# A graph network's first layer in one pass over a symmetric adjacency, with its batch norms as affine maps

## The chip, the cores and the metric

The kernel runs on one core of a Trainium2 chip. The metric is the time on the device in microseconds (us), the median of several executions. The engines are named as in the profile: PE multiplies matrices (PEld is its loading of weights), DVE is the vector engine, ACT the scalar engine, POOL GpSimd, and SP the engine that issues most of the DMA transfers. Each engine works through its own instructions in a fixed order and waits on semaphores for the others.

## The reference, cut to what matters

There are B = 16 batches of N = 1024 nodes with D = 128 features. `adj` is a matrix of 0 and 1 for each batch; it is drawn at random, made symmetric, and has ones on its diagonal. Four layers follow each other; each ends in a residual and a layer norm over the features.

```python
# layer 0
w = masked_row_softmax(transpose(adj))       # equal shares over the neighbours
region = w @ x
region = batch_norm(region @ kernel_1 + bias_1)      # over batches and nodes, 256 features
people = transpose(w) @ region
people = batch_norm(people @ kernel_2 + bias_2)      # over batches and nodes, 128 features
x = layernorm(x + people)
# layer 1: h = x @ W + b_W;  e[i,j] = leaky_relu(s1[i] + s2[j] + b_a)
#          softmax over i of where(adj > 0, e), relu, residual, layer norm
# layers 2, 3: scores[i,j] = leaky_relu(sum_d h[i,d] a[d] h[j,d]) where adj == 1,
#              softmax over j, times h, residual, layer norm
```

Because the entries are 0 and 1, the softmax of layer 0 gives 1/degree at each neighbour. The batch norms need the mean and variance over all 16 batches before any batch can go on.

## The kernel before

`fast_path` computes all four layers; a flag `bad`, gathered from checks on the data (that adj holds 0 and 1 only, and that the sums of the softmaxes lie in bounds), starts `general_path` if one fails. The order of each engine's queue is fixed when the program is built: a scheduler walks through the operations in the order in which the Python code calls them, with the buffers and PSUM slots of the tile pools deciding what can stand early. In the names, C = 8 is the number of 128-row blocks of a batch, H = 2 and G = 2 are halves of 512 columns and groups of four blocks, and A = 129.

Layer 0 takes two sweeps over the batches. In the first, each batch loads x (L510), splits it into a high and a low half in the matmul's rounded type (L512 on ACT, L513 on DVE), loads eight rows of adj of 512 KB (SP) and casts them to a mask `m` (`cast_mask`: every third on ACT, L461, the others on DVE, L463). 64 matmuls (L523) with blocks of the mask as weights add up the neighbours of each node, the degree in one more column; L526 to L530 divide, L535 transposes, L536 copies into `hid`, which stays in SBUF for all batches, and L540 and L542 take the statistics of the first batch norm. `batch_norm_affine` turns them into a scale and a shift, which are folded into one matrix `k12` and one row `c12` (L544 to L565). In the second sweep each batch forms `hid` times `k12` (L574), adds and divides (L577, L579), splits again (L583, L584), loads eight rows of `adjt`, the transpose of adj laid out on the host, casts them to a mask, and sums with 32 matmuls of 512 columns (L593). `people` goes to DRAM, transposed, with a bias (L598, statistics L600, store L601 on ACT's queue). The second batch norm follows.

Layers 1 to 3 are in the class `Batch`. Even batches form one stream and odd ones another, three phases behind; the phases `first`, `first_sum`, `other`, `other_sum`, `other`, `other_sum` of the two streams are laced together by the position of each step in its phase. Buffers carry the stream's number, and most exist once per stream, `x0` among them. The phase `first` is the entry of layer 1:

- `load` (L676, L678): x0 and the batch's people, `pe`, from DRAM;
- `people_norm` (L681): the second batch norm as one ACT operation on the transposed people;
- `add_transposed` (L657, L658): eight transposes on PE into PSUM, two additions on DVE with x0 into `res`; `collect` (L637, L638) takes the moments of each of the eight blocks;
- `apply`: the layer norm. `rsqrt` has two operations on POOL (L443, L444), then L644 on DVE and eight ACT operations L648; `rows_of` transposes the result (L667, L669);
- `scores1` (L695, L696, L697), `values1` (L706, L708, L711) and eight steps `weights1`, each with a row of `adjt` from DRAM (L715), ACT's L717 and DVE's L721 and L723.

Beside it runs, in the other stream, an `other_sum` or `other` phase with its matmuls L758 or L748 and the exponentials L753.

## Time and profile before

| | |
|---|---|
| time, median of 3 (range) | 2398.34 us (2398.07 to 2401.47) |
| time of the profiled execution | 2401.34 us |
| its span | 2399.5 us |
| busy PE, DVE, ACT, POOL | 78%, 68%, 41%, 6% of the span |
| granted PE clock, mean | 0.891 |
| 0 to 270 us: PE, DVE, ACT busy; DMA share; GB/s | 228.05, 194.09, 109.45 us; 0.89; 305 |
| 270 to 480 us: the same | 172.06, 137.60, 70.15 us; 0.94; 339 |
| read from memory, written | 226.90 MB, 16.78 MB |

The page cuts the span into 40 equal slices of 60 us; a digit is the busy share in tenths. The slices of the DMA row separate layer 0 from the rest. A row of the timeline gives the start in us, the busy time, the engine and line, the operation with its output and inputs, the tile's shape, how many instructions the row holds, and in brackets how long the engine had been idle and what released it. PE's ends are modelled, so the duration of one matmul is best taken from the distance between neighbours in a row of many.

### The profile page before, as it was taken

How to read it: one execution, taken by the hardware profiler on the slowest of the kernel's cores; microseconds unless marked ns; L12 is line 12 of the kernel's file. 1: busy time of each engine (PE TensorE's matmuls, PEld its weight loads, DVE VectorE, ACT ScalarE, POOL GpSimd, SP SyncE). 2: the span in 40 equal slices, each digit the busy share in tenths (PEclk: the TensorE clock that was granted, in tenths of full speed). 3: DMA queues.
4: the chain of work that ended last, by engine and by line, in shares of the span. 5: the costliest groups of instructions: out<-in, count | busy, mean ns of one | idle time of the engine just before them, and what ended most of it. 6: DMA issues, size and time to landing. Idle time of an engine off the chain costs nothing.

```text
span 2399.5 us, 24698 instructions
## 1 busy us (share of the span) xinstructions
PE 1874.0 (78%) x8661; PEld 1255.8 (52%) x8661; DVE 1626.4 (68%) x3714; ACT 981.9 (41%) x1577; POOL 150.5 (6%) x220
## 2 busy tenths in 40 slices
PE   6999888647787877868696969696868787878786
PEld 5776765425363645454554545454545454645464
DVE  5777776546575858575857676676758585767664
ACT  3444333333444444444444344444434343535332
POOL 0000000000000000000101010100000000000000
PEclk9999999968888989898888989898989898889887
DMA  8999899931111212020203030303030202020100
GB/s 288 315 309 319 281 343 359 347 118 39 49 54 43 64 33 79 19 76 22 88 9 97 1 97 0 97 1 97 1 97 14 84 27 70 9 71 10 44 9 11
DMA packets 110951, 245.39 MB, mean 102 GB/s; under 512 B 7776, under 2 KB 57568, under 8 KB 110816
## 3 DMA queue, kind: packets, MB, share of 16 engines
q1 hardware_dynamic: 108512, 235.31, 29.2%
q10 hardware_dynamic: 2304, 8.39, 0.9%
q8 instruction: 71, 1.16, 0.2%
q14 instruction: 64, 0.52, 0.1%
HBM read 226.90 MB, written 16.78 MB: 102 GB/s over the span
## 4 chain that ended last, share of the span: by engine, by line
DVE 44%; PE 30%; ACT 9%; DMA 6%; issue 5%; POOL 4%; SPq 0%; ACTq 0%; POOLq 0%
PE pacc L737 10%; PE pbig L748 4%; DMA at<-in_adjt_dram 4%; DVE ln_st L637 4%; PE pz L523 4%; PE pacc L758 3%; DVE m L463 2%; PE pt L667 2%; PE pr L540 2%; PE pbig L695 1%; PE pacc L706 1%; POOL rs_t L443 1%; PE pz L593 1%; DVE rs L763 1%; DMA at<-in_adj_dram 1%
## 5 line engine op out<-in xcount | busy, mean ns | idle before, releaser
L523 PE MATMUL pz<-x,m 128*128 128x258 f32 x1024 | 163.1, 307 | 27.9 <-DVE reg L530 18.1
L463 DVE CAST m<-at 128x1024 fp32r<-128x1024 int32 x192 | 131.2, 684 | 73.4 <-DMA at<-in_adjt_dram 58.7
L523 PEld LDWEIGHTS pz<-x,m 128*128 128x128 f32 x1024 | 137.8, 199 | 52.3 <-DVE reg L530 26.2
L593 PE MATMUL pz<-m,x 128*128 128x512 f32 x512 | 144.9, 419 | 25.6 <-DVE m L463 15.7
L762 DVE TENSOR_SCALAR sums<-pacc 128x1 f32<-128x1 f32 x256 | 37.7, 147 | 150.5 <-PE pacc L758 149.2
L593 PEld LDWEIGHTS pz<-m,x 128*128 128x128 f32 x512 | 92.0, 194 | 66.0 <-DVE m L463 33.1
L461 ACT CAST m<-at 128x1024 fp32r<-128x1024 int32 x64 | 67.0, 1047 | 71.3 <-DMA at<-in_adjt_dram 69.0
L529 ACT ACTIVATE lo<-pz,rdeg 128x128 f32<-128x128 f32 x128 | 42.0, 366 | 106.6 <-DVE degs L526 74.6
L542 DVE BATCH_NORM_STATS2 stats<-pr 128x6 f32<-128x512 f32 x64 | 44.5, 696 | 30.7 <-PE pr L540 30.7
L540 PE MATMUL pr<-hid,k_sb 128*128 128x512 f32 x128 | 64.9, 618 | 0.3 <-ACT hid L536 0.3
L530 DVE SCALAR_TENSOR_TENSOR reg<-pz,rdeg,lo 128x128 f32<-128x128 f32 x128 | 40.5, 346 | 8.9 <-ACT lo L529 8.5
L598 ACT ACTIVATE reg<-pz,vec 128x512 f32<-128x512 f32 x32 | 20.2, 684 | 62.0 <-PE pz L593 62.0
L574 PE MATMUL pr<-k,hid 128*128 128x128 f32 x256 | 37.6, 290 | 7.6 <-DVE xf L577 7.6
L763 DVE RECIPROCAL rs<-sums 128x1 f32<-128x1 f32 x256 | 40.2, 159 | 4.7
L574 PEld LDWEIGHTS pr<-k,hid 128*128 128x128 f32 x256 | 35.7, 202 | 13.3 <-issue 7.0
L751 DVE TENSOR_TENSOR e__4340<-pbig,pen__4339 128x1024 f32<-128x1024 f32 x16 | 19.1, 1211 | 26.4 <-PE pbig L748 26.4
L737 PE MATMUL pacc<-e__4340,hn__4348 128*128 128x512 f32 x32 | 15.8, 655 | 21.4 <-DVE hn__4348 L730 21.4
L536 ACT COPY hid<-zt 128x512 f32<-128x512 f32 x32 | 18.7, 586 | 33.5 <-PE zt L535 33.5
L751 DVE TENSOR_TENSOR e__6601<-pbig,pen__6600 128x1024 f32<-128x1024 f32 x16 | 19.2, 1206 | 19.0 <-PE pbig L748 19.0
L751 DVE TENSOR_TENSOR e__5325<-pbig,pen__5324 128x1024 f32<-128x1024 f32 x16 | 19.2, 1205 | 18.9 <-PE pbig L748 18.9
L751 DVE TENSOR_TENSOR e__9153<-pbig,pen__9152 128x1024 f32<-128x1024 f32 x16 | 19.2, 1203 | 18.8 <-PE pbig L748 18.8
L751 DVE TENSOR_TENSOR e__10429<-pbig,pen__10428 128x1024 f32<-128x1024 f32 x16 | 19.2, 1203 | 18.7 <-PE pbig L748 18.7
(1313 smaller groups left out, 5057.2 us busy)
## 6 DMA issues: line engine op xcount, KB each, us to landing
at<-in_adj_dram SPq DMA_DIRECT2D x128, 512.0 KB, 5.8
at<-in_adjt_dram SPq DMA_DIRECT2D x128, 512.0 KB, 5.6
adjt<-in_adjt_dram SPq DMA_DIRECT2D x128, 512.0 KB, 3.6
xf<-in_x_dram SPq DMA_DIRECT2D x16, 512.0 KB, 7.6
people<-reg ACTq DMA_DIRECT2D x16, 512.0 KB, 6.0
x__4267<-in_x_dram SPq DMA_DIRECT2D x1, 512.0 KB, 4.5
x__4548<-in_x_dram SPq DMA_DIRECT2D x1, 512.0 KB, 6.8
pe__4269<-people SPq DMA_DIRECT2D x1, 512.0 KB, 3.3
```

Source lines behind the costliest of these rows:

```text
L461: nc.scalar.copy(dst, src)
L463: nc.vector.tensor_copy(dst, src)
L523: nc.tensor.matmul(pz[:, :2 * D + 2], m[:, i, j * P:(j + 1) * P], x2[:, i, :], start=(i == 0), stop=(i == C - 1))
L540: nc.tensor.matmul(pr, k1_sb[:, s * P:(s + 1) * P], hid[b][:, h * 512:(h + 1) * 512], start=True, stop=True)
L574: nc.tensor.matmul(pv[:, k * P:(k + 1) * P], hid[b][:, c * P:(c + 1) * P], k12, start=True, stop=True)
L593: nc.tensor.matmul(pp[h], v2[:, c, s, :], mt[:, c, h * 512:(h + 1) * 512], start=(c == 0 and s == 0), stop=(c == C - 1 and s == 1))
L637: nc.vector.bn_stats(st, self.res[:, c, :])
L737: nc.tensor.matmul(po, self.hn[:, c, :D], self.e[:, c, h * 512:(h + 1) * 512], start=(c == 0), stop=(c == C - 1))
L748: nc.tensor.matmul(ps[:, cols], self.xw[:, c * P:(c + 1) * P], self.xt[:, cols], start=True, stop=True)
L751: nc.vector.tensor_tensor(e, ps, self.pen[:, c, :], ALU.subtract)
L758: nc.tensor.matmul(po[:, :A], self.e[:, m, c * P:(c + 1) * P], self.xl[:, m, :], start=(m == 0), stop=(m == C - 1))
L763: nc.vector.reciprocal(rs, total)
```

## The change

Layer 0 becomes one pass over adj, in a class `Pass` with two phases per batch; the second phase of a batch is laced with the first of the next one by `in_turn`.

The first phase loads x and splits it as before, loads the eight rows of adj and casts each on ACT, where the same operation sums the row into `degs`. The mask is now what is streamed (32 matmuls of 512 columns, into two PSUM tiles `z`), so that the sums come out transposed. `compare` checks on the chip that adj is symmetric: 36 blocks per batch are transposed by a matmul with an identity, and DVE counts the elements in which they differ from the mirrored block (12 operations). A difference would make `bad` start the general path.

The second phase copies z to SBUF, transposes it back and divides by the degrees (`region`), multiplies the region by its own transpose into a running PSUM sum (`moment1`), divides once more and splits (`split`), and sums over the neighbours with 64 matmuls of 258 columns which use the same mask (`back`). The result `g` (129 columns: the 128 features and the sum of the weights) takes part in a second running sum (`moment2`) and goes to DRAM.

Since kernel_1, the batch norms and kernel_2 are affine maps, they are applied after the sums: when all batches are through, the covariance of the regions gives the first norm's scale and shift, the moments of g the second's, and all of it becomes a matrix `k12s`, a row `c12s` and a row `shift2s`. At the entry of layer 1 each batch loads g, POOL adds `shift2s` to x0, g is transposed (`people_rows`) and multiplied by `k12s`, and `add_people` adds the product and g's last column times `c12s` to x0. `people_norm` and the transposes of `pe` are gone.

```diff
-    people = dram.tile([B, P, N], F32, name="people")
+    people = dram.tile([B, P, C, A + 1], F32, name="people")
...
+    def affine(scale, shift, var, mean, gamma, beta):
...
+    with tc.tile_pool(name="z_load", bufs=4) as zl, tc.tile_pool(name="z_mask", bufs=3) as zm, \
+            tc.tile_pool(name="z_work", bufs=2) as zw, \
+            tc.tile_pool(name="z_sum", bufs=1, space=PSUM) as zs, \
+            tc.tile_pool(name="z_acc", bufs=2, space=PSUM) as za, \
+            tc.tile_pool(name="z_tr", bufs=2, space=PSUM) as zt, \
+            tc.tile_pool(name="z_gram", bufs=1, space=PSUM) as zg:
...
+            def add(self, i):
+                at = zl.tile([P, N], I32, name="at")
+                nc.sync.dma_start(at, adj[self.b, i * P:(i + 1) * P, :])
+                nc.scalar.activation(self.m[:, i, :], at, AF.Copy,
+                                     accum_out=degs[:, self.b, i:i + 1])
+                for s in range(2):
+                    for h in range(H):
+                        nc.tensor.matmul(self.z[h], self.x2[:, i, s, :],
+                                         self.m[:, i, h * 512:(h + 1) * 512],
+                                         start=(i == 0 and s == 0), stop=(i == C - 1 and s == 1))
+            def compare(self, j):
+                for k0 in range(0, j + 1, 4):
+                    n = min(4, j + 1 - k0)
+                    pt = zt.tile([P, 512], F32, name="zt")
+                    for k in range(n):
+                        nc.tensor.matmul(pt[:, k * P:(k + 1) * P],
+                                         self.m[:, k0 + k, j * P:(j + 1) * P], identr,
+                                         start=True, stop=True)
+                    junk = zw.tile([P, 512], BF16, name="junk")
+                    nc.vector.scalar_tensor_tensor(
+                        junk[:, :n * P], pt[:, :n * P], 1.0,
+                        self.m[:, j, k0 * P:(k0 + n) * P].bitcast(F32), ALU.mult, ALU.not_equal,
+                        accum_out=unlike[:, self.b, j, k0 // 4:k0 // 4 + 1])
+            def rows(self):
...
+                for h in range(H):
+                    nc.scalar.copy(self.zt[:, h * 512:(h + 1) * 512], self.z[h])
...
+            def region(self, g):
...
+            def moment1(self, c):
+                nc.tensor.matmul(moments1[:, :A + 1], self.reg[:, c, :D], self.reg[:, c, :],
+                                 start=(self.b == 0 and c == 0),
+                                 stop=(self.b == B - 1 and c == C - 1))
+            def split(self):
...
+            def back(self, c):
+                pz = za.tile([P, 512], F32, name="pz")
+                for j in range(C):
+                    nc.tensor.matmul(pz[:, :2 * A], self.m[:, j, c * P:(c + 1) * P],
+                                     self.v2[:, j].rearrange("p s a -> p (s a)"),
+                                     start=(j == 0), stop=(j == C - 1))
+                lo = zw.tile([P, A], F32, name="lo")
+                nc.scalar.copy(lo, pz[:, A:2 * A])
+                nc.vector.tensor_tensor(self.g[:, c, :A], pz[:, :A], lo, ALU.add)
...
+            def store(self):
+                nc.vector.bn_stats(wstats[:, self.b, :], self.g[:, :, D])
+                nc.scalar.dma_start(people[self.b], self.g)
...
+        last = []
+        for b in range(B + 1):
+            first, second = Pass(b).phases() if b < B else ([], [])
+            in_turn(last, first)
+            last = second
...
             def load(self):
                 self.x0 = self.tile(rows, [P, C, D], F32, "x0")
                 nc.sync.dma_start(self.x0, x[self.b].rearrange("(c p) d -> p c d", p=P))
-                self.pe = self.row("pe")
-                nc.sync.dma_start(self.pe, people[self.b])
-
-            def people_norm(self):
-                nc.scalar.activation(self.pe, self.pe, AF.Identity, bias=shift2, scale=scale2)
+                self.g = self.tile(rows, [P, C, A + 1], F32, "g")
+                nc.sync.dma_start(self.g, people[self.b])
+                nc.gpsimd.tensor_tensor(
+                    self.x0, self.x0, wide["shift2s"][:, None, :].to_broadcast([P, C, D]), ALU.add)
                 self.new_norm()
+                self.gt = self.row("xt")
+
+            def people_rows(self, g):
+                pt = ps_tr.tile([P, 512], F32, name="pt")
+                for k in range(4):
+                    nc.tensor.transpose(pt[:, k * P:(k + 1) * P], self.g[:, 4 * g + k, :D], ident)
+                nc.scalar.copy(self.gt[:, g * 512:(g + 1) * 512], pt)
+
+            def add_people(self, g):
+                pt = ps_tr.tile([P, 4, P], F32, name="pt")
+                for k in range(4):
+                    c = 4 * g + k
+                    nc.tensor.matmul(pt[:, k, :], self.gt[:, c * P:(c + 1) * P], wide["k12s"],
+                                     start=True, stop=True)
+                    nc.vector.scalar_tensor_tensor(self.x0[:, c, :], wide["c12s"],
+                                                   self.g[:, c, D:A], self.x0[:, c, :], ALU.mult,
+                                                   ALU.add)
+                nc.vector.tensor_add(self.res[:, 4 * g:4 * g + 4, :], pt,
+                                     self.x0[:, 4 * g:4 * g + 4, :])
+                for k in range(4):
+                    self.collect(4 * g + k)
```

In the changed file the new lines of layer 0 are L505 (cast with degrees), L509 (z), L519 and L523 (`compare`), L535 (copies of z), L543 and L545 (`region`), L550 and L577 (the two running sums), L557, L560 and L561 (`split`), L569, L573 and L574 (`back`), L582 and L583 (`store`), L632 to L732 (the affine maps). At the entry of layer 1 they are L800 and L802 (loads), L803 (POOL's add), L811 and L812 (`people_rows`), L818, L820 and L823 (`add_people`). Later lines only move: L443 and L444 keep their numbers, L648 becomes L772, L695 becomes L839, L706 L850, L708 L852, L753 L897, L758 L902.

## The prediction

> **What bounds the kernel now.** I read the page's slices first, then the table of stretches, then the timeline of one cycle of each stage, and last the DMA issues.
>
> ```profile
> span 2399.5 us, 24698 instructions
> PE   6999888647787877868696969696868787878786
> DVE  5777776546575858575857676676758585767664
> PEclk9999999968888989898888989898989898889887
> DMA  8999899931111212020203030303030202020100
> ```
>
> The DMA row splits the span: eight slices (480 us, layer 0) at eight or nine tenths, then almost none. The stretches say the same; the columns are the stretch, its length, busy time of PE, PEld, DVE, ACT and POOL, granted clock, DMA share and GB/s.
>
> ```profile
> 120.00:180.00 60.00, 54.46 (x316) 42.11 (x316) 45.33 (x141) 26.15 (x52) 0.45 (x4) 0.97 0.91 309
> 360.00:420.00 60.00, 48.77 (x218) 34.05 (x219) 38.86 (x58) 18.22 (x21) 0.00 (x0) 1.00 0.97 358
> 800.00:1000.00 200.00, 155.62 (x689) 99.76 (x688) 136.96 (x314) 84.13 (x135) 16.50 (x22) 0.89 0.18 58
> ```
>
> So layer 0 is paid twice for the adjacency at 91 to 97% of the DMA engines (about 30 us per batch, both sweeps), with PE close behind. Layers 1 to 3 have a free DMA, and PE 78% and DVE 68% busy: no engine is full, so hand-overs between in-order queues bound them. One of these hand-overs is what the change touches, at the entry of layer 1 of an even batch:
>
> ```profile
> 924.00 2.28 ACT L753 ACTIVATE e__5963<-e__5963,shift 128x1024 f32<-128x1024 f32 x2 [0.30 <-DVE e__5963 L752]
> 925.01 1.28 DVE L658 TENSOR_TENSOR res__6469<-pt,x__6462 128x512 f32<-128x512 f32 x2
> 926.32 0.38 SPq L676 DMA_DIRECT2D x__7738<-in_x_dram  x1
> 929.78 0.20 POOL L443 TENSOR_SCALAR rs_t<-ln_mv__6470 128x8 f32<-128x8 f32 x1 [2.40 <-DVE ln_mv__6470 L638]
> 930.06 1.64 POOL L444 TENSOR_TENSOR ln_rstd__6523<-rs_t,neg_half 128x8 f32<-128x8 f32 x1
> 932.07 3.19 ACT L648 ACTIVATE xl__6529<-res__6469,ln_off__6527,ln_rstd__6523 128x128 f32<-128x128 f32 x8 [1.57 <-DVE rs L763]
> 935.77 1.98 PE L695 MATMUL pbig<-xt__6555,wa_rep 128*128 128x512 f32 x4
> 938.46 1.79 DVE L708 TENSOR_TENSOR hn__6609<-pacc,bw_row 128x387 f32<-128x387 f32 x3 [3.08 <-PE pacc L706]
> ...
> 1052.68 3.78 PE L695 MATMUL pbig<-xt__7193,wa_rep 128*128 128x512 f32 x4
> ```
>
> The reader is to see a single chain: residual (L658, ends 926.29), moments, POOL's rsqrt (L443, L444), ACT's apply (L648), PE (L695), DVE (L708, after 3.08 us idle). DVE and PE have nothing else in front in their queues, so a late L443 moves everything. The last row is the same four matmuls at half the granted clock: 3.78 us against 1.98. And the load of the x of the batch after next in this stream goes out at 926.32, the moment L658 has freed the buffer (one x0 buffer per stream).
>
> **Part 1, the loop of layer 0.** Removed: 128 loads of 512 KB (67 MB; at 339 GB/s some 200 us of transfer), the second casts, L535, L540, L574. Added: symmetry test (36 matmuls, 12 DVE operations per batch) and gram matrices. DMA per batch falls to 8 rows, x and people: ten times 1.66 us (512 KB at 315 GB/s), about 16.6 us. PE per batch, from the spacing inside rows of one group:
>
> ```profile
> 137.20 2.19 PE L523 MATMUL pz<-x,m 128*128 128x258 f32 x16
> 299.89 2.84 PE L574 MATMUL pr<-k,hid 128*128 128x128 f32 x24
> 309.38 9.56 PE L593 MATMUL pz<-m,x 128*128 128x512 f32 x38
> ```
>
> 258 columns: .127; 512: .248; fp32 of 128 columns: two instructions of .112, .224. Not in the trace is an fp32r 128x128 matmul on its own; bounds .063 (.127 halved with the columns) and .224 (fp32); I take the transposes' .11 (L535). 32x.248 + 64x.127 + 36x.11 + 8x.11 + 16x.224 = 24.5 us (23.5 with median spacings). ACT: 8 casts with accumulated degrees, for which L717 (1024 columns, accumulated) issues every 1.13 us, beside plain casts of 1.05 and 1.33 with the read-out not overlapped; I take 1.14: 9.1, plus x and v casts 2.1, z copies 1.2, eight lo .37: 17 us. DVE 14.5. So PE's sum is the floor, not DMA's.
>
> But batch b+1's sums and batch b's second phase are laced in fixed queues, and I follow the hand-overs. In the built program's queues, after z is summed: z copies .59+.59 (L536's row) and the x cast 1.06 on ACT; on DVE the low half of x 1.23 stands ahead of the last comparison's .75, and region's second group needs the PSUM slot which that comparison holds; two regions .68+.68 (L577's row), a comparison .35, v 1.23, ACT's v copy 1.05, low half of v 1.22: 9.4, with some .5 of semaphores 9.9. Then PE: 64 back matmuls 8.13, 7 z matmuls 1.74, 9 comparison matmuls .99: with .28 of fill 11.1. Then ACT, whose last five casts stand behind the last lo: .37 + 5x1.14 + .33 (people's issue), the last with a row that is only asked for when the fourth buffer is free: 6.5 to 7.5 before the next z copy. Sum 27.5 us per batch; the bounds are the dense floor 23.5 and, with the comparisons at .224, the casts at 1.33 and .2 more per hand-over, 30.5.
>
> First z copy: first cast 9.9 us, then DMA and eight rows, 27.5. Then 15x27.5 = 412, 440. Tail: no next batch to lace (regions to v 7.6, back 8.1, lo and moment2 1.5, less 3): 454. The batch-norm chains behind the last gram matrix are some 45 dependent small operations, .16 to .56 each (DVE .16, POOL .56 by L444's one-column row, PE fp32 about .43) : 15 to 17.5; 471. Store and first loads of people lie beside these. L811 to L823 (eight transposes, two .59 copies, eight .224 matmuls, add): 6.5, so the first residual is done at about 478, against
>
> ```profile
> 488.31 0.69 DVE L658 TENSOR_TENSOR res__4272<-pt,x__4267 128x512 f32<-128x512 f32 x1 [8.82 <-PE pt L657]
> ```
>
> Gain 10 us; ends -61 (23.5 per batch) and +35 (30.5).
>
> **Part 2, the entry of layer 1.** Removed per batch: people_norm on ACT 1.24 and 8 transposes. Added: L811, two copies of .59, eight matmuls of .224, eight DVE operations L820 (nearest L530 .35, L557 .28; 2.4 us in all) and one POOL add over 128x1024 (L803). L820 I cost at nothing: DVE idles 1.89, 1.09 and 3.08 us in the stretch shown; were that cover gone, 16x2.4 = 38 us.
>
> L803 is the matter. The add for batch b+2 stands in POOL's queue ahead of batch b's own L443, for b = 1, 2, 4, 6, 8, 10, 12. It waits for the load of x, which waits for batch b's L823 to free the buffer. So L443 of b waits for: L823 (its copies stand before the two last exponentials, whose sum matmuls stand before L818: 926.28 + two copies 1.18 + four sums .71 + the last four L818 .9 + the add .66 + some .6 of semaphores = 930.3 instead of 926.29, +4.1); the load, 4.65 by this row
>
> ```profile
> x__7738<-in_x_dram SPq DMA_DIRECT2D x1, 512.0 KB, 4.7
> ```
>
> (bounds 3.9 and 5.3, the other x loads); the add. No row shows a POOL add of this size: lower bound L513 on DVE, 1.2; upper 3.3, twice the whole of L444, POOL's longest; I take 2.3, between, as POOL's small operations run .20 to 1.64 where DVE's run .16 to .17. Against the present 3.5 from L658's end to L443: 4.1 + 4.65 + 2.3 - 3.5 = 7.6. PE's idle grows by as much, so L695 and L706 behind it go at half clock, some 1.6 of the row above's 1.8; one sum group fewer on DVE behind it saves 1.1. Per batch 7.5 to 8, seven batches 52 to 57. The last even batch, 14, has no b+2: +3. Odd ones (7) put the copies and matmuls beside sums: .5 each, 3.5. Layers 1 to 3: +59.
>
> The Trainium skill's "GPSIMD Engine Reference", section 3.1, measures a two-input add of 2048 fp32 columns at 4497 ns on GpSimd against 2293 on VectorE; halved, an estimate of 2.25 us for L803, and it speaks against the placement. No run here shows it yet. "TensorE: Matmul & The Clock Gate", Part 1, has the half clock come after about 3.4 us of idle; by that rule the wait of L443 costs clock as well as time, and so might the 9.9 us of hand-overs in each cycle of layer 0.
>
> **Sum.** 59 - 10 = +49. The profiled execution took 2401.34 us (span 2399.5 and 1.8 around it), 3.0 above the median of 2398.34; so 2450 for its like, 2447 against the median. Own range 2425 to 2475.
>
> **Rivals.**
> Faster: layer 0 becomes dense on PE. If the laced matmuls fill the 9.9 us, the cycle is 23.5 and saves 60 more: 2387. It decides from a cycle of 24.2 us (27.5 - 49/15) down. For it: PE is 54.46 of 60 busy in sweep one today; against it: region needs z whole and PE may run only three rows ahead. Chance .17.
>
> PE drops to half clock in every cycle of layer 0: the wait before the back matmuls holds some 4 us of PE work in 9.9. Price, one slow stretch of 1.7 to 3.4, 2.5x15 = 38: 2485. Chance .15. Against: clock 0.97 today.
>
> The POOL wait is mostly hidden (x lands early, or other work is drawn forward): 3 instead of 7.6 per batch, 21+6.5-10: 2416. Chance .15. Against: queues are in order and DVE's gaps show nothing to draw.
>
> The symmetry test fails and the general path runs: its loads alone, four times 67 MB at 343 GB/s, are 780 us: over 3200. Chance .01; adj is made symmetric with ones on the diagonal.
>
> **Chances and range.** Forecast .52, rivals as given. Faster by over 0.2% (5 us, what a measurement of this kernel can tell from none) .17: the first rival; same .04, from edges of it and the third; slower .79. The range 2385 to 2495 takes in all but the farthest of the first two rivals and the last.
>
> **What would show it.** Layer 0: z copies 27.5 us apart, PE share there about 85%, DMA share near 0.55, first L823 near 478. Entry: L803 right ahead of L443 with its releaser the x load, L443 about 7 to 8 us later after L823 than L658 now, L839 at about 3.8 us. Wrong if z copies come every 24 us, if L443 does not wait for L803, or if L820 shows on the chain.

## The result and the profile after

The changed kernel takes 2461.73 us (median of 4, 2460.2 to 2463.38) against 2398.72 us of the kernel before on the same chip: a ratio of 1.0261, 95% interval 1.0243 to 1.0278. It is slower by 63 us; 2447 were forecast, within 2385 to 2495. The profiled execution took 2463.38 us, its span 2461.6.

The slices of the page, as before in 40 parts, now of 61.5 us:

```profile
span 2461.6 us, 26764 instructions
PE   7898999566968686868686868686868687878786
DVE  4545555456767676767576757675767575857674
PEclk9999999677989797979797979797979797989887
DMA  9656542122020202020202020202020202020100
```

The reader should see that the DMA row falls to 5 and 4 within layer 0, that PE stands at 9 there, and that layer 0 is hardly shorter. DVE's digits in layer 0 fall to 4 and 5, since the casts have gone to ACT.

Where the time went is read from the first residual of layer 1 (L658 before, L823 after), which divides the span. Rows of the timeline:

```profile
471.58 0.68 DVE L823 TENSOR_TENSOR res__4758<-pt,x__4753 128x512 f32<-128x512 f32 x1
```

It came at 488.31 before and comes at 471.58 now. Layer 0 and its affine maps thus give back 16.7 us; what follows takes 2461.6 - 471.6 = 1990.0 instead of 1911.2, which is 78.8 more. The net of +62 is the sum of these two. In layers 1 to 3 two batches (one of each stream) make one period, read from one even batch's first L823 to the next one's: 245.1 us on average over six periods against 232.8.

**Layer 0.** One line of the copies of z gives the first and last of 32 (two per batch), and the table of stretches has the same stretch as before:

```profile
L535 ACT COPY ztr<-z x32: 564/586/592, 25.8 to 423.4; 128x512 f32<-128x512 f32 x32
```

```profile
120.00:180.00 60.00, 54.93 (x396) 50.46 (x395) 29.98 (x90) 28.43 (x61) 0.45 (x4) 1.00 0.52 176
```

The second copy of a pair starts 0.5 after the first, so (422.9 - 25.8)/15 = 26.5 us per batch, at a DMA share of 0.52 and a full clock; PE is busy 92%. The hand-overs of one cycle, from the timeline:

```profile
188.13 1.05 ACT L535 COPY ztr<-z 128x512 f32<-128x512 f32 x2
188.75 0.66 PE L543 MATMUL zt<-ident,ztr 128*128 128x128 f32 x4 [0.56 <-ACT ztr L535]
190.16 1.23 DVE L497 TENSOR_TENSOR x<-xf,x 128x1024 fp32r<-128x1024 f32 x1 [1.68 <-ACT x L496]
191.91 1.53 DVE L545 TENSOR_TENSOR reg<-zt,r 128x512 f32<-128x512 f32 x2
192.06 0.66 PE L543 MATMUL zt<-ident,ztr 128*128 128x128 f32 x4 [1.26 <-DVE junk L523]
195.91 1.23 DVE L561 TENSOR_TENSOR v<-v,v 128x1032 fp32r<-128x1032 f32 x1 [0.46 <-ACT v L560]
197.21 1.23 PE L569 MATMUL pz<-v,m 128*128 128x258 f32 x8 [0.40 <-DVE v L561]
```

From the z copies to the first back matmul 9.1 us pass, and the order is the one described in the prediction: the low half of x (L497) ahead of the comparison and of region, the second transposes released by a comparison (L523).

**The entry of an even batch.** The rows answer to those shown of before:

```profile
925.19 0.69 DVE L823 TENSOR_TENSOR res__7037<-pt,x__7032 128x512 f32<-128x512 f32 x1 [0.35 <-PE pt L818]
925.96 0.38 SPq L800 DMA_DIRECT2D x__8350<-in_x_dram  x1
930.22 2.34 POOL L803 TENSOR_TENSOR x__8350<-x__8350,shift2s 128x1024 f32<-128x1024 f32 x1 [4.25 <-DMA x__8350<-in_x_dram]
932.64 0.20 POOL L443 TENSOR_SCALAR rs_t<-ln_mv__7038 128x8 f32<-128x8 f32 x1
934.61 0.17 DVE L768 SCALAR_TENSOR_TENSOR ln_off__7134<-ln_mv__7038,ln_rstd__7130 128x8 f32<-128x8 f32 x1 [4.27 <-POOL ln_rstd__7130 L444]
936.06 0.42 PE L791 MATMUL pt<-ident,xl__7136 128*128 128x128 f32 x1
```

L823 ends at 925.88, the next x is asked for at once, lands at 930.2, is added to, and only then L443 runs: 6.8 us after L823, where 3.5 us lay between L658 and L443 before. All seven batches concerned (1 and the even ones from 2 to 12) show 6.7 to 6.9; batch 14, which has no successor, 3.6. The last row is a transposition: 0.42 us here, 0.27 before (L667). PE had waited 3.96 us ahead of the first of these; its granted clock was 0.63 from 937 to 942 us, where the kernel before has 1.00 from 936 to 941.

**The entry of an odd batch**, which the prediction had priced at 0.5 us:

```profile
1053.64 0.20 POOL L443 TENSOR_SCALAR rs_t<-ln_mv__7697 128x8 f32<-128x8 f32 x1 [3.30 <-DVE sums L906]
1055.53 2.34 POOL L803 TENSOR_TENSOR x__9009<-x__9009,shift2s 128x1024 f32<-128x1024 f32 x1
1055.59 2.29 DVE L768 SCALAR_TENSOR_TENSOR ln_off__7793<-ln_mv__7697,ln_rstd__7789 128x8 f32<-128x8 f32 x1 [1.81 <-POOL ln_rstd__7789 L444]
```

Here L443 is in time, but L768, an operation on eight columns that took 0.17 us in the even batch, takes 2.29 us: it starts 0.06 us after POOL's add and ends with it. This happens in five odd batches (3 to 11), in each of which L803 starts just ahead of L768. Batch 13 is the comparison, since x came later there and L768 began ahead of the add:

```profile
2038.64 0.17 DVE L768 SCALAR_TENSOR_TENSOR ln_off__13065<-ln_mv__12969,ln_rstd__13061 128x8 f32<-128x8 f32 x1 [1.81 <-POOL ln_rstd__13061 L444]
2038.99 2.37 POOL L803 TENSOR_TENSOR x__14281<-x__14281,shift2s 128x1024 f32<-128x1024 f32 x1 [0.38 <-DMA x__14281<-in_x_dram]
```

The period with this batch took 242.4 us, the five with a blocked L768 245.4 to 245.8, though the even batch waited on POOL in all six. A blocked L768, with what stands behind it, thus costs 3.0 to 3.4 us, and the five cost some 17. Two kernels described below have the same code in layers 1 to 3 (without the test, and with other slots for region). Their traces agree: 242.4 or 242.5 us in the three periods in which L768 took 0.17, 245.4 to 245.8 in the other nine.

### The profile page after: what moved, and what is told of

The parts are those of the page before. It is cut to its first block, busy times and chain, and to the rows that moved or that the text cites. A ratio compares the mean times of both kernels' runs of the same rounds, so it can differ in the third digit from the quotient of the medians.

```text
span 2461.6 us, 26764 instructions
## 1 busy us (share of the span) xinstructions
PE 1934.0 (79%) x9645; PEld 1388.7 (56%) x9645; DVE 1572.2 (64%) x3737; ACT 1024.7 (42%) x1761; POOL 182.5 (7%) x252
## 4 chain that ended last, share of the span: by engine, by line
DVE 38%; PE 35%; ACT 11%; issue 6%; POOL 5%; DMA 5%; SPq 0%; ACTq 0%; POOLq 0%
PE pacc L881 10%; PE pacc L902 6%; PE pz L569 5%; PE pbig L892 5%; DMA at<-in_adj_dram 4%; DVE ln_st L761 3%; PE pt L791 3%; PE z L509 1%; PE pacc L850 1%; ACT m L505 1%; PE pbig L839 1%; POOL rs_t L443 1%; DVE rs L907 1%; PE zt L519 1%; DVE e__14441 L895 1%
## 5 line engine op out<-in xcount | busy, mean ns | idle before, releaser
L509 PE MATMUL z<-m,x 128*128 128x512 f32 x512 | 155.3, 417 | 10.8 <-ACT m L505 10.8
L569 PE MATMUL pz<-v,m 128*128 128x258 f32 x1024 | 140.8, 289 | 8.9 <-DVE v L561 7.8
L505 ACT ACTIVATE m<-at 128x1024 fp32r<-128x1024 int32 x128 | 134.4, 1055 | 26.7 <-DMA at<-in_adj_dram 25.5
L569 PEld LDWEIGHTS pz<-v,m 128*128 128x128 f32 x1024 | 132.1, 192 | 16.0 <-DVE v L561 12.2
L523 DVE SCALAR_TENSOR_TENSOR junk<-zt,m 128x512 bf16<-128x512 f32 (+1 forms) x192 | 102.2, 552 | 56.9 <-PE zt L519 54.2
L574 DVE TENSOR_TENSOR g<-pz,lo 128x129 f32<-128x129 f32 x128 | 37.3, 292 | 109.8 <-ACT lo L573 109.8
L509 PEld LDWEIGHTS z<-m,x 128*128 128x128 f32 x512 | 89.4, 192 | 21.7 <-ACT m L505 10.8
L573 ACT COPY lo<-pz 128x129 f32<-128x129 f32 x128 | 34.1, 267 | 146.6 <-PE pz L569 146.6
L519 PE MATMUL zt<-identr,m 128*128 128x128 f32 x576 | 85.3, 275 | 1.0 <-DVE junk L523 1.0
L519 PEld LDWEIGHTS zt<-identr,m 128*128 128x128 f32 x576 | 75.3, 192 | 3.1 <-DVE junk L523 2.1
L550 PE MATMUL moments<-reg 128*128 128x130 f32 x256 | 43.3, 284 | 0.3 <-DVE reg L545 0.3
L577 PE MATMUL moments<-g 128*128 128x130 f32 x256 | 42.5, 281 | 0.0
L543 PE MATMUL zt<-ident,ztr 128*128 128x128 f32 x128 | 20.7, 284 | 26.0 <-DVE junk L523 17.9
L577 PEld LDWEIGHTS moments<-g 128*128 128x128 f32 x256 | 38.0, 190 | 3.9
L497 DVE TENSOR_TENSOR x<-xf,x 128x1024 fp32r<-128x1024 f32 x16 | 19.6, 1225 | 30.7 <-ACT x L496 30.7
L550 PEld LDWEIGHTS moments<-reg 128*128 128x128 f32 x256 | 36.9, 190 | 2.6 <-issue 0.5
L895 DVE TENSOR_TENSOR e__4847<-pbig,pen__4846 128x1024 f32<-128x1024 f32 x16 | 19.2, 1216 | 25.5 <-PE pbig L892 25.5
L543 PEld LDWEIGHTS zt<-ident,ztr 128*128 128x128 f32 x128 | 13.6, 140 | 34.2 <-DVE junk L523 21.8
L895 DVE TENSOR_TENSOR e__7192<-pbig,pen__7191 128x1024 f32<-128x1024 f32 x16 | 19.2, 1207 | 19.9 <-PE pbig L892 19.9
```

The costliest lines, as they stand in the source:

```text
L505: nc.scalar.activation(self.m[:, i, :], at, AF.Copy, accum_out=degs[:, self.b, i:i + 1])
L509: nc.tensor.matmul(self.z[h], self.x2[:, i, s, :], self.m[:, i, h * 512:(h + 1) * 512], start=(i == 0 and s == 0), stop=(i == C - 1 and s ...
L519: nc.tensor.matmul(pt[:, k * P:(k + 1) * P], self.m[:, k0 + k, j * P:(j + 1) * P], identr, start=True, stop=True)
L523: nc.vector.scalar_tensor_tensor(junk[:, :n * P], pt[:, :n * P], 1.0, self.m[:, j, k0 * P:(k0 + n) * P].bitcast(F32), ALU.mult, ALU.not_equal,
L550: nc.tensor.matmul(moments1[:, :A + 1], self.reg[:, c, :D], self.reg[:, c, :], start=(self.b == 0 and c == 0), stop=(self.b == B - 1 and c ...
L569: nc.tensor.matmul(pz[:, :2 * A], self.m[:, j, c * P:(c + 1) * P], self.v2[:, j].rearrange("p s a -> p (s a)"), start=(j == 0), stop=(j == ...
```

## The experiments

Medians are given with the ratio to the kernel before measured beside them; the changed kernel has 1.0261. The kernel before lay between 2396.95 and 2400.48 us beside these runs. "Period" is the average of six periods of two batches as above, read from the profiled execution. Four of the kernels ("Both rows by PE", "Cheaper matmuls", "Two x0 buffers", "An adjacency taken as symmetric") also write one small tile of the checks at the end (`zeros`) into the tile `checks`; no run has that alone.

### Without POOL's add

```diff
-                nc.gpsimd.tensor_tensor(
-                    self.x0, self.x0, wide["shift2s"][:, None, :].to_broadcast([P, C, D]), ALU.add)
```

> POOL's add L803 is left out altogether, so the row shift2s is missing from the result; everything else is as in the changed kernel (2461.7 us). Theory (the add's place costs an even batch its wait, L443 6.8 us after L823 where 3.5 belong, with cold matmuls behind, and it blocks DVE for 2.3 us in odd batches): L443 comes 3.5 us after L823 in even batches, L768 takes 0.17 us everywhere, 6 to 7 us per pair of batches, seven pairs 42 to 49 and 2 more at the start: 2410 to 2418. Rival (the entry is long because of the copies, the eight matmuls and the sum groups that moved, and the add merely stands in time that is lost anyway): 2445 or more, with other rows as the releasers of L768.

Measured: 2412.07 us, ratio 1.0068 (1.0051 to 1.0085). The period is 237.2 us. The entry of the same even batch, which now comes some 15 us earlier:

```profile
910.52 0.69 DVE L821 TENSOR_TENSOR res__7032<-pt,x__7028 128x512 f32<-128x512 f32 x1 [0.35 <-PE pt L816]
914.80 0.20 POOL L443 TENSOR_SCALAR rs_t<-ln_mv__7033 128x8 f32<-128x8 f32 x1 [3.51 <-DVE sums L904]
916.76 0.17 DVE L768 SCALAR_TENSOR_TENSOR ln_off__7129<-ln_mv__7033,ln_rstd__7125 128x8 f32<-128x8 f32 x1 [1.75 <-POOL ln_rstd__7125 L444]
```

(This kernel has two lines less; L821 is the residual.) L443 follows 3.6 us after it. The add costs 49.7 us of the 78.8: 7.9 per period. The other 4.4 per period stay, with nothing of the add left. L768 takes 0.17 us in every batch here.

### The residual written in place

```diff
-                self.new_norm()
+                self.res = self.x0
+                self.mv = self.tile(small, [P, C, 2], F32, "ln_mv", bufs=2)
```

> L823 writes its sum into x0 instead of a tile of its own, so x0 comes free only after the layer norm's L772; the load of the next x, and with it POOL's add, falls behind this batch's L443 and L444. The add stays as long as it was. Theory of the wait alone: all of it goes, as in the run without the add: 2410 to 2420. Theory that the add also blocks DVE's instructions with two operands in SBUF while it runs: the 2.3 us come back once per batch wherever it lands (L865 takes up to 3.5 us once instead of 1.25), half to all of 15 times 2.1 us more than without the add: 2425 to 2445.

Measured: 2449.04 us, ratio 1.0214 (1.0195 to 1.0234); period 241.8. L443 follows the residual by 3.7 us in the even batches, so the wait on POOL is gone, but only 12.7 us came back, less than either theory gave. The timeline shows why, and it is neither of the two:

```profile
936.21 0.38 SPq L800 DMA_DIRECT2D x__8344<-in_x_dram  x1
940.08 0.56 DVE L853 TENSOR_TENSOR hn__7211<-pacc,bw_row 128x387 f32<-128x387 f32 x1
940.49 2.34 POOL L803 TENSOR_TENSOR x__8344<-x__8344,shift2s 128x1024 f32<-128x1024 f32 x1 [7.78 <-DMA x__8344<-in_x_dram]
942.87 0.35 DVE L821 SCALAR_TENSOR_TENSOR x__8344<-c12s,g__8346,x__8344 128x128 f32<-128x128 f32 x1 [2.03 <-POOL x__8344 L803]
943.23 0.86 DVE L853 TENSOR_TENSOR hn__7211<-pacc,bw_row 128x387 f32<-128x387 f32 x2
```

(L821 is L820 of the changed kernel.) In DVE's queue the first update of the next x stands between the parts of this batch's L853, and it needs the result of the add: DVE waits 2.03 us for it, with PE's sums behind. In the odd batch that follows the same wait is 0.72 us. A wait that was taken off POOL's queue came back in DVE's. Over the six periods the two waits make 2.9 us on average, of the 4.6 by which the period stays above that of the run without the add; the rest is not assigned. The same rows show that here DVE was not held up by the add running beside it, as L768 was: it had nothing but this dependent instruction to run.

### The row added by PE

```diff
-                nc.gpsimd.tensor_tensor(
-                    self.x0, self.x0, wide["shift2s"][:, None, :].to_broadcast([P, C, D]), ALU.add)
...
                 pt = ps_tr.tile([P, 4, P], F32, name="pt")
+                nc.tensor.matmul(pt, ones[0:1, :],
+                                 wide["shift2s"][0:1, None, :].to_broadcast([1, 4, D]),
+                                 start=True, stop=False)
...
-                                     start=True, stop=True)
+                                     start=False, stop=(k == 3))
```

> The row shift2s is added on PE: one matmul of 512 columns with a single row of ones as weights opens each of the two PSUM tiles of add_people, and POOL's add is gone. Theory: as without the add, plus at most two such matmuls of 0.86 us per batch, if they stand on the path, 0 to 26 us: 2412 to 2440, near 2420 because they wait for nothing but the PSUM slot. Rival (the add's place does not matter): no better than 2450.

Measured: 2432.55 us (2426.51 to 2440.2), ratio 1.016 (1.0132 to 1.0187); period 239.0. It gives back 29 of the 49.7 us, within the range stated but not at 2420. (The profiled execution is the fastest of the four.) The extra matmuls stand on the path:

```profile
913.63 1.12 PE L814 MATMUL pt<-shift2s,ones 1*128 1x512 f32 x2 [1.19 <-ACT xt__7042 L810]
914.68 0.94 PE L819 MATMUL pt<-k12s,xt__7042 128*128 128x128 f32 x6
```

L814 reads nothing that is late, and still begins only when ACT's copies L810 are through: the PSUM slot that it opens is one that L810 empties, and the products L819 stand behind it.

### Without the symmetry test

```diff
-                yield steps(self.load, *[(f, i) for i in range(C) for f in (self.add, self.compare)])
+                yield steps(self.load, *[(self.add, i) for i in range(C)])
```

> The symmetry test (36 matmuls and 12 DVE operations per batch of layer 0) is left out; its counters stay zero. If PE's own work sets the cycle of layer 0 (26.5 us, PE busy 0.92): 36 times 0.11 less per cycle, 4.0 us, 15 cycles 60: about 2400. If the hand-overs set it: 0.75 and 0.35 us of DVE leave the wait and 1.0 us leaves the stretch of the back matmuls, 2.1 to 2.6 us per cycle, 32 to 39: 2423 to 2430. If casts and DMA set it: nothing, 2461.

Measured: 2371.2 us, ratio 0.9894 (0.9877 to 0.991), 90 us less than the changed kernel. More than the largest of the three expectations. The same two views:

```profile
120.00:180.00 60.00, 59.32 (x403) 53.84 (x402) 23.05 (x48) 40.05 (x83) 0.68 (x6) 1.00 0.76 258
```

The cycle is 20.6 us and PE is busy 59.32 of 60. With the prediction's spacings the work left per batch is 24.5 - 36 x .11 = 20.5: layer 0 without the test is bound by PE alone. So the test costs 5.9 us per cycle: 4.0 as PE's work, by those spacings, and 1.9 beyond it. That these 1.9 are hand-overs which the test causes is likely, and not shown. The first residual came at 378.6 instead of 471.6. The period stayed near 245, so the two stages are independent.

### Region in other PSUM slots

```diff
             def region(self, g):
-                pt = zt.tile([P, 512], F32, name="zt")
+                pt = za.tile([P, 512], F32, name="pz")
```

> Only the PSUM pool of region's transposes changes: they use the two slots of the back matmuls instead of those that the symmetry test holds. In the changed kernel the second group of transposes starts 3.3 us after the first, released by a comparison. Theory (hand-overs still cost 1.9 us of the 26.5 us cycle beyond PE's own 24.6, and this slot is the largest of them): the two groups follow each other within 1.5 us, the cycle falls to 24.6 to 25.5, 15 to 28 us less: 2434 to 2447. Rival (PE is full, the wait is covered by other matmuls): cycle 26.3 or more, 2458 to 2463.

Measured: 2458.13 us, ratio 1.0229 (1.0204 to 1.0255); cycle 26.7 us, while two kernels measured beside it that have the changed kernel's layer 0 as it was show 26.8 and 26.9. The rival holds for the time: the gain is lost. The eight transposes now come as one row, and region (L545) still starts 3.2 us after they begin, because on DVE the low half of x and a comparison stand ahead of it. The wait moved from PE's slot to DVE's order.

### The next x split later

```diff
+            def hold(self):
+                held = small.tile([P, 1], F32, name="held")
+                nc.gpsimd.tensor_tensor(held, self.x2[:, 0, 0, 0:1].bitcast(F32),
+                                        self.g[:, 2, 0:1], ALU.add)
...
-                            *[(self.back, c) for c in range(C)],
+                            *[(self.back, c) for c in range(3)], self.hold,
+                            *[(self.back, c) for c in range(3, C)],
```

(with the load and split of x in a step of their own, late in the previous batch, and region in the slots of the run above)

> As region_za, and in addition the split of the next x is moved: a small POOL operation (one column) that reads x2 and the third block of g keeps the x2 buffer taken until the back matmuls are under way, so the x cast (ACT 1.06) and the low half (DVE 1.23) leave the stretch between the z copies and the back matmuls, and ACT makes four casts there instead of three. Theory (the DVE queue holds region back, not PE): z copies to back falls from 9 to about 7 us, back's end to the next z copies from 6.6 to 5.5, and PE's own 24.6 us becomes the limit: cycle 24.6 to 25.3, 20 to 30 us less than the changed kernel: 2433 to 2443. Rival (PE's work with its gaps at DVE's comparisons is the limit): cycle stays at 26.4 or more, 2455 or more.

Measured: 2452.09 us, ratio 1.0235 (1.0214 to 1.0255); cycle 26.1 us. The split did move among the back matmuls and PE rose to 56.77 of 60 in the stretch from 120 to 180 us, but the cycle missed the 24.6 to 25.3 that I expected. The cycles are uneven, and the long ones are those in which an adjacency row arrives late ahead of v's cast. Of the ten ordinary cycles from the fifth on, the four in which ACT waited 1.0 to 1.3 us for such a row took 26.3 to 28.3 us, the six others 25.1 to 25.5. (In the changed kernel ACT has such a wait in almost every cycle, ahead of the z copies.) Why the rows come late in some cycles only was not looked for. What would bring layer 0 to PE's floor with the test in it is left open.

### POOL with one operand

```diff
-                nc.gpsimd.tensor_tensor(
-                    self.x0, self.x0, wide["shift2s"][:, None, :].to_broadcast([P, C, D]), ALU.add)
+                nc.gpsimd.tensor_scalar(self.x0, self.x0, 0.0, None, ALU.add)
```

> POOL's add of x0 and the row shift2s becomes an add of the constant zero to x0, so it reads one operand and the row is missing from the result; its place in the queues and its wait for x stay. Theory that POOL's operation with two operands blocks DVE's operations with two SBUF operands: L768 takes 0.17 us in every batch instead of 2.29 in odd ones, and odd batches give back some 2 us each; with the add itself perhaps a microsecond shorter in even ones, 2435 to 2450. Theory that any POOL operation of this size blocks DVE: L768 stays as long as POOL's operation. Theory that L768 was long for another reason: it stays 2.29.

Measured: 2448.98 us, ratio 1.0203 (1.0179 to 1.0227); period 242.3. In the same odd batch:

```profile
1055.57 2.78 POOL L803 TENSOR_SCALAR x__9009<-x__9009 128x1024 f32<-128x1024 f32 x1
1055.63 0.99 DVE L768 SCALAR_TENSOR_TENSOR ln_off__7793<-ln_mv__7697,ln_rstd__7789 128x8 f32<-128x8 f32 x1 [1.81 <-POOL ln_rstd__7789 L444]
```

POOL's operation became longer (2.78 against 2.34), and DVE's blocked one shorter (0.99 against 2.29). None of the three theories is met exactly: L768 is still blocked, but not for POOL's recorded span. A POOL span is rough, so how long the operation really read is not known; what is shown is that the length of L768 follows what POOL does beside it, and not its own eight columns. The period is 2.9 us shorter although the wait of even batches grew to 7.0 to 7.4 us, which agrees with the 3.0 to 3.4 us that a blocked L768 was seen to cost above. In batches 11 and 13 of this run L768 began ahead of POOL's operation and took 0.17 us, and their periods (242.2 and 242.3) are those of the others: the shorter hold of 0.99 us costs nothing that can be seen.

### Without L820 as well

```diff
-                    nc.vector.scalar_tensor_tensor(self.x0[:, c, :], wide["c12s"],
-                                                   self.g[:, c, D:A], self.x0[:, c, :], ALU.mult,
-                                                   ALU.add)
```

> The run without POOL's add (2412.1 us), and in addition without the eight DVE operations L820 per batch: g's last column times c12s is missing from the result too. The prediction costed L820 at nothing because DVE idles where it lies: then 2407 to 2412. If its 2.4 us per batch lie on the path: 16 times 2.4 is 38, about 2374; in between the covered part can be read off.

Measured: 2414.99 us, ratio 1.0057 (1.0038 to 1.0076), and period 237.2, against 1.0068 and 237.2 with L820. Where POOL's add is gone, the 128 operations cost nothing that can be measured. No run leaves them out with the add in place.

### Both rows by PE

```diff
+                nc.tensor.matmul(pt, self.wt[:, g, :], rows8, start=True, stop=False)
                 for k in range(4):
                     c = 4 * g + k
                     nc.tensor.matmul(pt[:, k, :], self.gt[:, c * P:(c + 1) * P], wide["k12s"],
-                                     start=True, stop=True)
-                    nc.vector.scalar_tensor_tensor(self.x0[:, c, :], wide["c12s"],
-                                                   self.g[:, c, D:A], self.x0[:, c, :], ALU.mult,
-                                                   ALU.add)
+                                     start=False, stop=(k == 3))
```

(`wt` holds g's two last columns, transposed; POOL's add is gone and region uses the other slots)

> Both rows (c12s and shift2s) are added by PE: g's two last columns are transposed to 8 rows per group, and one fp32 matmul of 512 columns with a block-wise constant opens each PSUM tile of add_people; POOL's add and L820 are gone, so nothing reads x0 before L823. Region's transposes use the slots of the back matmuls as in region_za. Theory: first L823 near 443 (cycle 24.6 to 25.5), a pair of batches 235 to 238 us instead of 245.5 (before: 233.9): 2355 to 2385. If the rest of the entry (copies and matmuls ahead of L823) is what costs, pairs stay above 240: 2400 or more.

Measured: 2432.9 us, ratio 1.0131 (1.0112 to 1.0151); period 239.0, first residual 474.8. Neither expectation holds. The period is that of the run with the row added by PE: to take L820 off DVE bought nothing, as the run above would have told, and the cycle of layer 0 did not fall.

### Cheaper matmuls for the row

```diff
+                for s in range(2):
+                    nc.tensor.matmul(pt, one_row, shift_row[:, s, None, :].to_broadcast([1, 4, D]),
+                                     start=(s == 0), stop=False)
```

(on top of the later split; `shift_row` holds the high and the low half in the rounded type)

> x_later, and POOL's add replaced by two matmuls of one row (the high and the low half of shift2s in the rounded type, 512 columns, 0.25 us each instead of the 0.86 of the fp32 one in shift_pe) that open each PSUM tile of add_people. Theory: layer 0 as in x_later, pairs of batches 237.5 to 238.5 us (237.3 without any add, 239.0 with the fp32 matmul, 245.5 with POOL's add): 48 to 55 less than x_later: 2380 to 2395, below the kernel before. If the shift's matmuls cost more by their PSUM slot than by their time, pairs stay at 239 and 2390 to 2400.

Measured: 2424.58 us, ratio 1.0114 (1.0094 to 1.0134); period 239.4, 238.9 without the first. The two matmuls that open a PSUM tile take 0.73 us from start to end where they follow each other at once, against 1.12 for the pair of instructions of the fp32 one. The period is the same as with the long ones, so their duration alone does not explain the 1.7 us per period. The expectation of 237.5 to 238.5 was wrong; the other one has the period (239), but not the time (2390 to 2400). Whether it is the PSUM slot or the place in PE's queue was not separated.

### Two x0 buffers for even batches

```diff
-                self.x0 = self.tile(rows, [P, C, D], F32, "x0")
+                self.x0 = self.tile(rows, [P, C, D], F32, "x0", bufs=2 - self.s)
```

> The changed kernel with two x0 buffers instead of one in the stream of the even batches. In its queues POOL's add of batch b+4 now stands where that of b+2 stood, ahead of L443 of batch b, and its x goes into the buffer that L823 of batch b frees. Theory (the add's place in POOL's queue is the cost, and a deeper buffer only fetches from further ahead): L443 stays 6 to 7 us after L823, 2455 to 2465. Rival (one buffer is the cost): the wait of even batches goes, 3 to 5 us each, 2425 to 2440.

Measured: 2460.81 us, ratio 1.0262 (1.0245 to 1.0279): no change, as the first theory has it.

```profile
926.54 0.38 SPq L800 DMA_DIRECT2D x__9668<-in_x_dram  x1
930.84 2.42 POOL L803 TENSOR_TENSOR x__9668<-x__9668,shift2s 128x1024 f32<-128x1024 f32 x1 [4.29 <-DVE rs L907]
933.34 0.20 POOL L443 TENSOR_SCALAR rs_t<-ln_mv__7038 128x8 f32<-128x8 f32 x1
```

The x that POOL adds to ahead of the same L443 is now x__9668, that of the batch after the next in this stream, and it waits for the buffer that this batch frees. The deeper buffer only moved the place that the queue runs ahead to: L443 stays 6.6 to 6.8 us after L823. In batch 12, for which the stream has no further x to add, it is 4.0 us, and the period is 242.3 instead of 245.8.

### An adjacency taken as symmetric

```diff
-                yield steps(self.load, *[(f, i) for i in range(C) for f in (self.add, self.compare)])
+                yield steps(self.load, *[(self.add, i) for i in range(C)])
```

(on top of the run with the cheaper matmuls)

> shift_r without the symmetry test: its counters stay zero, so the result would be wrong for an adjacency that is not symmetric. The two measured gains add up if they lie in different stages: the run without the test was at 2371.2, the shift by PE took 29 off the changed kernel: 2340 to 2350, faster than the kernel before by 2%. If layer 0's gain is paid back at the entry of layer 1: 2370.

Measured: 2351.42 us, ratio 0.981 (0.9794 to 0.9826), just above the range of the first expectation; the first residual comes at 388.9. The gains of the two stages add up, less 10 us: with the moved split the cycle without the test is 21.3 instead of 20.6. This is faster than both kernels, at the price of the test; with the test in it, no version here was faster than the kernel before.

## Why the prediction was right, and where its sizes were off

**Direction and mechanism.** The forecast was slower, by a gain of 10 in layer 0 and a loss of 59 behind it; measured are 16.7 and 78.8. The two misses have opposite signs, 6.7 and 19.8 us, so it is partly luck that the total lies within 15 us of the forecast.

The mechanism named first, POOL's add ahead of L443 and behind the load of the next x, is shown by the row of L803 with its releaser and by the run without the add. That run takes 1940.4 us behind its first residual, against 1990.0 with the add and 1911.2 before: the add costs 49.6 of the 78.8, the rest of the entry 29.2. Some 17 of the 49.6 are the blocked L768, which the prediction did not have; that leaves 33 for the wait on POOL in seven batches, 4.7 each, if the two add up. The prediction had 35 for this wait (seven times 5.05), nothing for the block, and 24 for the rest. Removing the wait in POOL's queue by other means (in place, two buffers) brought back 12.7 us and nothing, since the same dependence then stood in DVE's queue, or one batch further.

**Layer 0, by its terms.** The first z copy came at 25.8 (27.5 predicted) and the cycle was 26.5 (27.5), of which z copies to back took 9.1 (9.9), the back stretch 10.6 (11.1), and back to the next copies 6.8 (6.5 to 7.5). The sum along the queues was thus the right way to count; PE's dense floor of 24.5 is what the test's removal confirmed, at 20.6 without it. Behind the loop two terms were too small, which took back 11 of the 17 us that the loop came out better. The tail from the last z copies to the last gram matrix took 20 us instead of 14: 64 back matmuls with nothing laced between them, 9.5 us, behind a region and split of 8. And the entry to the first residual took 11.4 us instead of 6.5, by these rows and the one of L823 above:

```profile
459.92 0.27 ACT L731 COPY shift2s<-zt 128x128 f32<-128x128 f32 x1 [9.01 <-DVE k12s L730]
460.03 0.38 SPq L800 DMA_DIRECT2D x__4753<-in_x_dram  x1
464.48 2.34 POOL L803 TENSOR_TENSOR x__4753<-x__4753,shift2s 128x1024 f32<-128x1024 f32 x1 [4.26 <-DMA x__4753<-in_x_dram]
466.86 4.28 DVE L820 SCALAR_TENSOR_TENSOR x__4753<-c12s,g__4755,x__4753 128x128 f32<-128x128 f32 x8 [6.97 <-DMA x__5055<-in_x_dram]
```

The step "Store and first loads of people lie beside these" failed: the first load is issued only when the chain of affine maps ends, 0.1 us after L730 has made k12s, for which SP had waited 15.4 us. The load does not read k12s; that its buffer lies in memory of layer 0's pools is the likely reason, and not shown. The add follows the load, and L820 the add. One of its eight operations took 2.43 us, from 0.09 us after the start of the next batch's add (467.56, 2.38 us) to 0.15 us past its end: the same hold as that of L768. The 6.5 us had neither the load, nor the add, nor L820 in them. The affine chain itself took 17.3 us, within the 15 to 17.5. Two sums of the prediction do not come out of their terms, though the forecast rests on neither: ACT's terms make 15.4 us and not 17, and 15 cycles of 23.5 us change layer 0 by -70 and not -61.

**Even batches.** Predicted were 7.5 to 8 us each, of which L803's part (load 4.65, add 2.3, less 3.5, clock 1.6) is 5.05. The load took 4.25 and the add 2.34, taken as 2.3 between bounds of 1.2 and 3.3 (the estimate of 2.25 was close too). From the end of L823 to L443 the wait grew by 3.3 us, as against 3.45 predicted. With DVE's instructions of an ordinary period (232.3 us before, 245.8 after) laid beside each other, the even batch is 6.5 us behind when the odd batch's entry begins. The half clock came, but not where the prediction said: L839 took 1.88 us at full clock in the batch shown, and it was L791 and the sums laced with it, ahead of L839, that ran at 0.42 and more. Their delay between L768 and L852 is 2.4 us (3.7 to 6.1 behind), against 1.6 predicted for the clock.

**Odd batches: the step that failed.** They were put at .5 us each, and lose 4.8 in the same period (11.3 us behind after the odd batch's entry, 6.5 ahead of it); another 2 us are spread over the rest of the period, unassigned. The prediction followed POOL's queue and found L443 ahead of L803 in odd batches; it did not ask what POOL's add does to DVE while it runs. L768 at 2.29 us instead of 0.17 is 2.1 of the 4.8, and with what stands behind it 3.4, by the period of batch 13; the run with one operand, in which it took 0.99, gave back 2.9 per period. The five periods with a blocked L768 make some 17 us, most of the 19.8 by which layers 1 to 3 came out worse than forecast.

A page of the Trainium skill states the rule that I did not apply: "SBUF — State Buffer", in "Who interferes with whom", says that a DVE instruction with two SBUF inputs contends with a GpSimd instruction that reads SBUF, and that the shared port pair is an exclusive lock. The trace agrees for L768, which has two SBUF operands (2.29 us beside the add, 0.17 alone), and for L908, which has one operand in PSUM and ran at 0.32 us while an add was under way. In the run with one operand L768 was held for 0.99 us of a recorded 2.78; by that page the whole recorded span would have been expected, and no run here shows when POOL's reading ended.

**L820 at nothing** was right for the periods as far as the runs show: without POOL's add, the run without L820 is the same to 0.1 us per period. At the first entry it was wrong: L820 stands on the path there with 4.28 us, once. **The rest of the entry** (copies, eight matmuls, the moved sum group) was put at 4.1 - 1.1 + .5, that is 3.5 us per pair; the run without the add shows 237.2 - 232.8 = 4.4.

**The rivals.** A PE-dense layer 0 would have needed a cycle of 24.2 and was at 26.5; it is where the kernel goes if the test is left out. The half clock in layer 0 did not come (1.00 in the stretch). The POOL wait was not hidden. The general path did not run.

## What to carry to other kernels

Where an engine's order is fixed when the kernel is built, an operation on data that arrives later costs most through what stands behind it: look in the queue of each engine for the instruction of the next stage that waits for a buffer which this stage frees, and do not count on a second buffer: here it only let the queue run further ahead. An add given to an idle engine need not be free: here it held an instruction of DVE with two operands in SBUF for 2.29 us, so ask which of the neighbour's instructions read two. And a check on the data, added to a stage, is to be priced against the stage's new bound: here DMA had been the bound (a share of 0.91 to 0.97), and the test's matmuls fell on PE, which took its place (busy 92% with the test, 99% without).

## What the runs showed of the hardware

A DVE instruction of 8 columns with two operands in SBUF took 2.29 us while a POOL add of two operands over 1024 columns was running (2.34 us), 0.99 us beside a POOL operation with one operand, and 0.17 us otherwise, also when it began only 0.05 us ahead of the add (with other slots for region, batch 13). A DVE instruction of 128 columns with two SBUF operands (L820) was held in the same way once, for 2.43 us. One with an operand in PSUM (L908) took its usual 0.32 us beside the add. POOL's two-operand add over 128x1024 fp32 took 2.34 to 2.38 us in all 16 executions in the changed kernel's trace; the addition of a constant to the same tile was recorded at 2.78. Opening a PSUM tile with two short matmuls (0.73 us together) instead of an fp32 one (1.12) left the period unchanged, 238.9 against 239.0.
